# A combined schedule change in a four-layer network kernel: layer 1's turn and MLP begin, and Fourier's row 64, last unit and second copy

## The chip, the cores and the metric

The kernel runs on one core of one Trainium2 chip. The metric is the device time of one execution in microseconds (us); lower is better. Everything is computed in one launch, in float32 unless the reference asks for rounding to a smaller format.

## The reference, cut to what matters

The network has four layers on an image batch of 4 x 96 channels x 64 x 64 (16,384 tokens of 96 channels, 4,096 per image). Layer 0 is a selective state-space block, and layer 2 is a linear attention with a quantised MLP; the change touches neither. Layer 1 and the first half of layer 3 are these:

```python
# layer 1
h = conv_depthwise_7x7(x) + conv_b                 # per channel
h = layer_norm_over_channels(h) * ln_g + ln_b
h = gelu(h @ w1 + b1)                              # 96 -> 384
x = (h @ w2 + b2) * layer_scale + x                # 384 -> 96
# layer 3, first half ("Fourier"); its input is layer-normed, its output added to t
h = relu(bn1(x @ w1.T))                            # 96 -> 192
X = fft(h, axis=tokens, norm="ortho")              # 4096 tokens
xr = relu(X.real * rd - X.imag * idg + rb)
xi = relu(X.imag * rd + X.real * idg + ib)
y = ifft(xr + 1j * xi, axis=tokens, norm="ortho").real
o = bn2(y @ w2.T)                                  # 192 -> 96
```

A second quantised MLP ends layer 3 and the kernel.

## The kernel before, in words

The stages run one after another. Through most of the kernel t, a tile of 96 partitions by 16,384 tokens, stays in SBUF. In layers 1 to 3 the order of instructions on TensorE (PE), VectorE (DVE), ScalarE (ACT) and GpSimd (POOL) is the program's order (a manual schedule). DMAs are issued on SyncE's queue (SP), whose order a planner of the framework sets; a DMA is issued when the queue has come to it and its slot is free. Tiles with a tag share a ring of `bufs` slots.

**Layer 1, the turn.** `tokens` loads 1,024 tokens of layer 0's output (`o`) and of the input (`xr`), scales the one on ACT and adds the other on DVE into t (L737). `turn` brings these tokens from channels on partitions to tokens on partitions: eight blocks of 128 tokens go in as TensorE's weights, and the moving operand is a unit matrix of 96 rows (L744). Four blocks share a PSUM tile, which ACT copies in one half and DVE in the other into xt. There are 16 chunks, and the tokens of a chunk are asked for one chunk ahead.

**Layer 1, the convolution.** It is done with banded matrices, 1 MB for four channels, loaded as `band`, three slots. At the eighth of 24 groups it also prepares constants for the later layers (`consts2`), whose small matmuls use the turn's PSUM ring.

**Layer 1, the MLP.** A block is 512 tokens; there are 32, in eight groups of four. `stats` takes mean and variance on DVE (four rows of 128 tokens per call), `roots` the inverse square root of a group's variances on ACT by Ln and Exp, `back` normalises on DVE and turns the block back on TensorE, `hidden` is the first matrix with Gelu on ACT, `out` the second, added to t on DVE. Ln and Exp, and Gelu, are in different function tables of ACT, and a table load stands between them.

**Fourier.** The transform over 4,096 tokens is split in 32 x 128. A unit is one image and one half of the 192 hidden features, so there are eight units; a unit takes four steps of six groups of features. In step j of the loop, `over_n1(j)` is the first transform (L1139) with the twiddle products on DVE and POOL, `over_n2(j - 1)` the second (L1160 to L1163) with the weights rd and id, `fold(j - 2)` the relu and the folding to frequencies 0 to 63, `over_k2(j - 3)` the first half of the inverse (L1208, L1209), copied by ACT into bt. `over_k1` is the second half (L1230), on blocks of four columns, with a piece of the inverse matrix loaded as gt (256 KB, two slots), a copy of its PSUM tile into ys by ACT (L1232), and `w2` (L1238) adds the product with the second weight to t on DVE. The inverse of a unit starts two units (eight steps) after its forward transform began; a step does two blocks.

Frequency 64 has its own path: `row64` makes that row by two small products and writes it into partition 64 of bt by way of DRAM, as two DMAs, one after the other (d<-r, bt<-d). The inverse of the unit can't start until it has landed.

```python
if (j - 7) % PER == 0 and 0 <= (j - 7) // PER < len(units):
    row64((j - 7) // PER)
```

Beside this, the units of even number prepare the layer norm of the next image (`norm1`, `norm2`), and those of odd number its first matmul with relu (`w1`, into hh, a ring of three slots). For the last image there is nothing more to prepare.

Of the kernel before, what the change touches and what calls it, by code (L numbers as in the profile page):

```python
# [9 lines left out]
F32 = mybir.dt.float32  # L10
# [8 lines left out]
B, C, HW, L = 4, 96, 64, 4096  # L19
# [31 lines left out]
class Net:  # L51
# [661 lines left out]
    def layer1(self, scratch, t):  # L713
# [4 lines left out]
        with ExitStack() as ctx:  # L718
# [4 lines left out]
            with (  # L723
                tc.manual_schedule(engines=engines),
                tc.tile_pool(name="l1a", bufs=1) as wk,
                tc.tile_pool(name="l1ap", bufs=1, space=PSUM) as psum,
            ):
                for at in (slice(0, 2), slice(NR + 2, NR + 4)):
                    nc.gpsimd.memset(xt[:, :, :, at], 0.0)
                def tokens(b, s):  # L730
                    at = slice(b * L + s * T, b * L + (s + 1) * T)
                    o = wk.tile([C, T], F32, name="o", tag="o", bufs=3)
                    nc.sync.dma_start(o, scratch[:, at])
                    xr = wk.tile([C, T], F32, name="xr", tag="xr", bufs=3)
                    nc.sync.dma_start(xr, ins["x"][b, :, s * T : (s + 1) * T])
                    nc.scalar.activation(o, o, AF.Identity, scale=self.osc, bias=self.osh)
                    nc.vector.tensor_add(t[:, at], o, xr)  # L737

                def turn(b, s):
                    for h in range(2):  # L740
                        ps = psum.tile([128, 4, C], F32, name="xt_ps", tag="xt", bufs=4)
                        for d in range(4):
                            a = b * L + s * T + (4 * h + d) * 128
                            nc.tensor.matmul(ps[:, d], t[:, a : a + 128], self.ident[:C, :C], start=True, stop=True)  # L744
                        r = 2 + s * (T // 128) + 4 * h
                        dst = xt[:, :, b, r : r + 4].rearrange("p c r -> p r c")
                        if h:
                            nc.vector.tensor_copy(dst, ps)
                        else:
                            nc.scalar.copy(dst, ps)  # L750

                chunks = [(b, s) for b in range(B) for s in range(NSC)]
                tokens(*chunks[0])
                for k, chunk in enumerate(chunks):
                    if k + 1 < len(chunks):
                        tokens(*chunks[k + 1])
                    turn(*chunk)

                def load(g):
                    w = wk.tile([128, GC, 4, 128], F32, name="band", tag="band", bufs=3)  # L760
                    nc.sync.dma_start(w, ins["band"][g])
                    return w

                def outer(g):

                    x2 = wk.tile([128, 2 * GC, B, NR], F32, name="x2", tag="x2", bufs=3)
                    at = slice(g * 2 * GC, (g + 1) * 2 * GC)
                    nc.gpsimd.tensor_copy(x2[:64], xt[:64, at, :, 4:])
                    nc.gpsimd.tensor_copy(x2[64:], xt[64:, at, :, :NR])
                    return x2  # L770

                def small(rows, cols):
                    ps = psum.tile([128, 4, C], F32, name="w_ps", tag="xt", bufs=4)
                    return ps.rearrange("p a c -> p (a c)")[:rows, :cols]

                x2 = [outer(0)]
                for g in range(C // GC):
                    if g == 8:
                        self.consts2(wk, small)
                    if g % 2 == 0 and g + 2 < C // GC:  # L780
                        x2.append(outer(g // 2 + 1))
                    w = load(g)
                    ps = psum.tile([128, GC, B, NR], F32, name="cv_ps", tag="cv", bufs=4)
                    for d in range(GC):
                        c = g * GC + d
                        for k, j in enumerate((1, 0, 2)):
                            nc.tensor.matmul(
                                ps[:, d], w[:, d, j], xt[:, c, :, 1 + j : 1 + j + NR], start=k == 0, stop=False
                            )
                        nc.tensor.matmul(ps[:, d], w[:, d, 3], x2[g // 2][:, g % 2 * GC + d], start=False, stop=True)  # L790
                    for d in range(GC):
                        c = g * GC + d
                        dst = xt[:, c, :, 2 : 2 + NR]
                        if g % 2:
                            nc.vector.tensor_scalar_add(dst, ps[:, d], cb[:, c : c + 1])
                        else:
                            nc.scalar.activation(dst, ps[:, d], AF.Identity, bias=cb[:, c : c + 1])
# [52 lines left out]
            n = NT // MB // 4  # L850
            with tc.manual_schedule(engines=engines):
                nc.scalar.preload_act_table_set(ACT_EXP_LN)
                for k in range(2):
                    for d in range(4):
                        stats(k, d)
                    roots(k)
                for d in range(4):
                    back(d)
                for k in range(n):
                    for d in range(4):  # L860
                        hidden(4 * k + d)
                        if k + 1 < n:
                            back(4 * k + 4 + d)
                        if k + 2 < n:
                            stats(k + 2, d)
                        if d:
                            out(4 * k + d - 1)
                    if k + 2 < n:
                        nc.scalar.preload_act_table_set(ACT_EXP_LN)
                        roots(k + 2)  # L870
                    out(4 * k + 3)
# [212 lines left out]
    def fourier(self, dram, t, h):  # L1084
# [5 lines left out]
        with ExitStack() as ctx:  # L1090
# [7 lines left out]
            def misc(rows):  # L1098
                return pln.tile([128, MB], F32, name="m_ps", tag="m", bufs=2)[:rows]
# [98 lines left out]
            def over_k2(i):  # L1198

                u, g = its[i]  # L1200
                z = zz.pop(i)
                if g == 0:
                    bt[u] = wk.tile([N1, N2, C], F32, name="bt", tag="bt", bufs=2)
                for e in range(0, G, 3):
                    ps = pln.tile([N1, 3, 128], F32, name="i1_ps", tag="i1", bufs=2)
                    for d in range(3):
                        zd = z[:, e + d].rearrange("p k m -> p (k m)")
                        nc.tensor.matmul(ps[:, d], zd[:, 64:], bc, start=True, stop=False)  # L1208
                        nc.tensor.matmul(ps[:, d], zd[:, :128], bs, start=False, stop=True)  # L1209
                    nc.scalar.copy(  # L1210
                        bt[u].rearrange("p n (g c) -> p g n c", c=4)[:, g + e : g + e + 3],
                        ps.rearrange("p g (n c) -> p g n c", c=4),
                    )

            def row64(u):
# [6 lines left out]
                nc.sync.dma_start(d.rearrange("o (n g c) -> g (o n) c", n=N2, c=4), r)  # L1222
                nc.sync.dma_start(bt[u][64:65].rearrange("p n c -> p (n c)"), d)

            def over_k1(u, n, kept):
                gt = wk.tile([N1, 4, N1], F32, name="gt", tag="gt", bufs=2)
                nc.sync.dma_start(gt, ins["idft"][:, n : n + 4])
                ps = misc(C).rearrange("p (n a) -> p n a", n=4)
                for d in range(4):
                    nc.tensor.matmul(ps[:, d], bt[u][:, n + d], gt[:, d], start=True, stop=True)  # L1230
                kept[u, n] = wk.tile([C, MB], F32, name="ys", tag="ys", bufs=2)
                nc.scalar.copy(kept[u, n], ps.rearrange("p n a -> p (n a)"))  # L1232

            def w2(u, n, kept):

                b, half = units[u]
                ps = misc(C)
                nc.tensor.matmul(ps, self.a_w2[:, half, :], kept.pop((u, n)), start=True, stop=True)  # L1238
                ps = ps.rearrange("p (n a) -> p n a", n=4)
                td = ft[b][:, n : n + 4]  # L1240
# [6 lines left out]
            with tc.manual_schedule(engines=engines):  # L1247
                for n in range(0, N2, 2):
                    w1(0, n)
                kept, sq = {}, {}  # L1250
                for j in range(len(its) + 12):
                    ub, k = divmod(j - 2 * PER, PER)
                    blocks = [(ub, n) for n in (8 * k, 8 * k + 4)] if 0 <= ub < len(units) else []

# [9 lines left out]

                    if j < len(its):
                        over_n1(j)

                    if normed:
                        norm1(b, a, sq)
# [18 lines left out]
                        over_k2(j - 3)  # L1288
                    if normed:
                        norm2(a, sq)  # L1290
                    if (j - 7) % PER == 0 and 0 <= (j - 7) // PER < len(units):
                        row64((j - 7) // PER)
                    turn(len(tokens))
                    if blocks:
                        w2(*blocks[1], kept)
                    if normed and k == PER - 1:
                        norm2(a + MB, sq)


def build(tc, ins, out):  # L1300
# [155 lines left out]
```

## Time and profile before

| | before |
|---|---|
| time, median of 3 runs | 3974.91 us (3973.95 to 3976.82) |
| profiled execution | 3972.29 us, its span 3970.5 us |
| PE, DVE, ACT, POOL busy, whole span | 83%, 79%, 61%, 73% |
| layer 1: turn, convolution, MLP | 2614 to 2670, 2670 to 2791, 2791 to 3014 us |
| Fourier | 3298 to 3838 us |
| last MLP | 3838 to 3970.5 us |

Times inside the execution are counted from the start of the span. "L744" is line 744 of the kernel. A busy TensorE isn't TensorE at its full rate: the profile also gives the clock that was granted to it, as a share of full speed. PEld is the load of weights, which runs beside the matmuls. An idle time of an engine has a releaser, the event that ended it; "issue" is time for which the profile shows no such event.

### The profile page before, as it was taken

How to read it: one execution, taken by the hardware profiler on the slowest of the kernel's cores; microseconds unless marked ns; L12 is line 12 of the kernel's file. 1: busy time of each engine (PE TensorE's matmuls, PEld its weight loads, DVE VectorE, ACT ScalarE, POOL GpSimd, SP SyncE). 2: the span in 40 equal slices, each digit the busy share in tenths (PEclk: the TensorE clock that was granted, in tenths of full speed). 3: DMA queues.
4: the chain of work that ended last, by engine and by line, in shares of the span. 5: the costliest groups of instructions: out<-in, count | busy, mean ns of one | idle time of the engine just before them, and what ended most of it. 6: DMA issues, size and time to landing. Idle time of an engine off the chain costs nothing. (4 is left out here: it accounts for less than half of the span.)

```text
span 3970.5 us, 45322 instructions
## 1 busy us (share of the span) xinstructions
PE 3291.6 (83%) x14174; PEld 1420.1 (36%) x14174; DVE 3155.9 (79%) x2772; ACT 2419.9 (61%) x4644; POOL 2912.9 (73%) x1443
## 2 busy tenths in 40 slices
PE   7888788888888778888878888677899998999878
PEld 3222222222222222222222222167445535666643
DVE  5999999999999999999999999941662384444539
ACT  4676667666666766677666666431345586655548
POOL 2999999999999999999999999911001064534417
PEclk8888888888887888788888888658899999999989
DMA  7567656756675667566666766566000000011111
GB/s 185 135 161 174 144 148 159 175 142 159 160 173 132 164 166 170 132 167 166 159 147 158 170 148 154 120 170 227 11 0 1 1 1 6 22 33 33 43 44 58
DMA packets 183291, 468.12 MB, mean 118 GB/s; under 512 B 53237, under 2 KB 55167, under 8 KB 179969
## 3 DMA queue, kind: packets, MB, share of 16 engines
q1 hardware_dynamic: 183048, 465.21, 47.1%
q8 instruction: 113, 1.85, 0.2%
q14 instruction: 130, 1.06, 0.1%
HBM read 391.53 MB, written 73.50 MB: 117 GB/s over the span
## 5 line engine op out<-in xcount | busy, mean ns | idle before, releaser
L496 POOL TENSOR_TENSOR hs<-hs,crep 128x1024 f32<-128x1024 f32 x768 | 1796.6, 2364 | 27.3 <-DVE hs L490 23.7
L454 PE MATMUL rep<-dbl,sel_b 32*128 32x512 f32 x1152 | 406.1, 781 | 464.1 <-DVE hs L490 433.4
L474 POOL TENSOR_TENSOR up<-udb,brep 128x1024 f32<-128x1024 f32 x256 | 605.1, 2364 | 8.5 <-DMA brep<-cd 8.5
L468 ACT ACTIVATE da<-ddb,nega 128x1024 f32<-128x1024 f32 x512 | 585.0, 1150 | 16.2 <-DVE hs L490 8.2
L468 ACT ACTIVATE dap<-ddb,nega 128x1024 f32<-128x1024 f32 x256 | 286.2, 1118 | 423.7 <-DVE hs L490 421.9
L515 PE MATMUL y<-hs,sel_r 128*32 128x512 f32 x3072 | 483.3, 689 | 6.5 <-POOL hs L496 6.4
L490 DVE TENSOR_TENSOR_SCAN hs<-da,state,rep 128x1024 f32<-128x1024 f32 x192 | 450.8, 2348 | 16.7
L490 DVE TENSOR_TENSOR_SCAN hs<-da,state,u 128x1024 f32<-128x1024 f32 x192 | 450.9, 2348 | 11.2 <-DVE u L486 1.4
L490 DVE TENSOR_TENSOR_SCAN hs<-dap,state,up 128x1024 f32<-128x1024 f32 x192 | 447.0, 2328 | 6.8 <-ACT dap L468 6.8
L454 PEld LDWEIGHTS rep<-dbl,sel_b 32*128 32x128 f32 x1152 | 109.0, 218 | 760.9 <-issue 512.8
L210 PE MATMUL ps<-n,w_x 97*64 97x512 f32 x1536 | 364.8, 617 | 9.4 <-ACT n L323 5.3
L486 DVE TENSOR_TENSOR u<-udb,rep 128x1024 f32<-128x1024 f32 x256 | 314.6, 1229 | 42.5 <-PE rep L454 11.3
L486 DVE TENSOR_TENSOR rep<-udb,rep 128x1024 f32<-128x1024 f32 x256 | 310.6, 1213 | 0.4
L1039 POOL CAST hq<-y 128x1536 fp8e5<-128x1536 f16 x64 | 93.9, 1467 | 253.7 <-issue 144.0
L210 PEld LDWEIGHTS ps<-n,w_x 97*64 97x64 f32 x1536 | 108.9, 140 | 257.5 <-issue 210.9
L515 PEld LDWEIGHTS y<-hs,sel_r 128*32 128x32 f32 x3072 | 66.9, 116 | 363.5 <-issue 195.8
L382 POOL TENSOR_TENSOR du<-delta,xc 128x512 f32<-128x512 f32 x96 | 122.6, 1277 | 67.4 <-ACT delta L366 52.2
L1178 POOL TENSOR_TENSOR av<-av,ec 128x780 f32<-128x780 f32 x32 | 58.8, 1837 | 150.1 <-ACT av L1175 150.1
L224 PE MATMUL ps<-xc,xproj 64*102 64x512 f32 x384 | 160.3, 998 | 3.5 <-ACT xc L344 3.5
L358 ACT COPY dbl<-ps 102x512 f32<-102x512 f32 x64 | 34.4, 589 | 207.1 <-PE ps L224 207.1
L911 POOL MEMSET h<- 1x4096 f32 x1 | 3.5, 3506 | 213.1 <-DVE n L824 213.1
L490 DVE TENSOR_TENSOR_SCAN hs<-da,rep 128x1024 f32<-128x1024 f32 x64 | 146.5, 2289 | 5.4
(256 smaller groups left out, 6492.9 us busy)
## 6 DMA issues: line engine op xcount, KB each, us to landing
ddb<-dd SPq DMA_DIRECT2D x768, 128.0 KB
udb<-ud SPq DMA_DIRECT2D x768, 128.0 KB
crep<-cd SPq DMA_DIRECT2D x512, 128.0 KB
brep<-cd SPq DMA_DIRECT2D x256, 128.0 KB
dd<-delta SPq DMA_DIRECT2D x64, 384.0 KB
ud<-du SPq DMA_DIRECT2D x192, 128.0 KB
band<-in_band SPq DMA_DIRECT2D x24, 1024.0 KB
gt<-in_idft SPq DMA_DIRECT2D x64, 256.0 KB
```

The source lines that it names most:

```text
L210: nc.tensor.matmul(ps[rows], w[:, 64 * p : 64 * p + 64], rhs[:, at.start + shift : at.stop + shift], start=k == 0, stop=k == len(ws) - 1, ...
L224: nc.tensor.matmul(ps, w[rows, p], x[rows, p], start=start and p == 0, stop=p == 2)
L382: nc.gpsimd.tensor_mul(u, m["delta"][:, of], m["xc"][:, of])
L454: nc.tensor.matmul(x[:, at], sel_b[rows, order[t][1]], made[k]["dbl"][rows, at], start=True, stop=True)
L468: nc.scalar.activation(da, made[k]["dd", h, j], AF.Exp, scale=nega[:, col : col + 1])
L474: nc.gpsimd.tensor_mul(u, made[k]["ud", h, j], made[k]["brep", g])
L486: nc.vector.tensor_mul(u, made[k]["ud", h, j], x)
L490: nc.vector.tensor_tensor_scan(hs[:, 1:], made[k].pop(("da", t)), u, 0.0 if s == 0 else st, ALU.mult, ALU.add)
L496: nc.gpsimd.tensor_mul(hs[:, :T], hs[:, 1:], made[k]["crep", order[t][1]])
L515: nc.tensor.matmul(made[k]["y", p][row : row + 32], sel_r, made[k]["hs", t][:, at], start=False, stop=True, skip_group_check=True,)
L1039: nc.gpsimd.tensor_copy(q, y2, saturate=False)
L1178: nc.gpsimd.tensor_add(v[:, 2:4], v[:, 0:2], ec)
```

## The change

Five things are edited:

- the turn's unit matrix is taken with all 128 columns, and its PSUM tiles, like those of the small constants and of `over_k2`, are made four by 128 wide, of which 96 or three parts are read;
- the begin of the MLP: the first group's statistics and roots, one `back`, and then the loop, in which the statistics of the second and third group and the second group's roots are spread over the first four blocks; `back` is now two blocks ahead of `hidden` instead of four;
- `row64` is called one step earlier;
- the last unit's blocks leave the loop; in a loop of their own, `over_k1` of a block comes ahead of `w2` of the block before, and `w2` there uses `over_k2`'s PSUM ring; the inverse matrix is loaded in two halves of 1 MB into slots of hh, and from there on no gt is loaded where a half holds it;
- ys of a step's second block is copied by DVE instead of ACT, but for the last unit.

```diff
 def turn(b, s):
     for h in range(2):
-        ps = psum.tile([128, 4, C], F32, name="xt_ps", tag="xt", bufs=4)
+        ps = psum.tile([128, 4, 128], F32, name="xt_ps", tag="xt", bufs=4)
         for d in range(4):
             a = b * L + s * T + (4 * h + d) * 128
-            nc.tensor.matmul(ps[:, d], t[:, a : a + 128], self.ident[:C, :C], start=True, stop=True)
+            nc.tensor.matmul(ps[:, d], t[:, a : a + 128], self.ident[:C], start=True, stop=True)
...
-                nc.vector.tensor_copy(dst, ps)
+                nc.vector.tensor_copy(dst, ps[:, :, :C])
             else:
-                nc.scalar.copy(dst, ps)
+                nc.scalar.copy(dst, ps[:, :, :C])
...
     nc.scalar.preload_act_table_set(ACT_EXP_LN)
-    for k in range(2):
-        for d in range(4):
-            stats(k, d)
-        roots(k)
     for d in range(4):
-        back(d)
+        stats(0, d)
+    roots(0)
+    back(0)
     for k in range(n):
         for d in range(4):
-            hidden(4 * k + d)
-            if k + 1 < n:
-                back(4 * k + 4 + d)
-            if k + 2 < n:
+            i = 4 * k + d
+            hidden(i)
+            if k == 0 and d == 2:
+                nc.scalar.preload_act_table_set(ACT_EXP_LN)
+                roots(1)
+            for i2 in (1, 2) if i == 0 else (i + 2,):
+                if i2 < 4 * n:
+                    back(i2)
+
+            if k == 0:
+                for d2 in (2 * (d % 2), 2 * (d % 2) + 1):
+                    stats(1 + d // 2, d2)
+            elif k + 2 < n:
                 stats(k + 2, d)
             if d:
-                out(4 * k + d - 1)
+                out(i - 1)
         if k + 2 < n:
             nc.scalar.preload_act_table_set(ACT_EXP_LN)
             roots(k + 2)
...
-    ps = pln.tile([N1, 3, 128], F32, name="i1_ps", tag="i1", bufs=2)
+    ps = pln.tile([N1, 4, 128], F32, name="i1_ps", tag="i1", bufs=2)[:, :3]
...
+late = {}
+
+def fetch(k):
+    g = wk.tile([N1, CG, N2, 4], F32, name="hh", tag="hh", bufs=3)
+    g = g.rearrange("p g n c -> p (g n c)")[:, : N2 // 2 * N1].rearrange("p (n a) -> p n a", n=N2 // 2)
+    nc.sync.dma_start(g, ins["idft"][:, k * N2 // 2 : (k + 1) * N2 // 2])
+    for n in range(0, N2 // 2, 4):
+        late[k * N2 // 2 + n] = g[:, n : n + 4]
+
 def over_k1(u, n, kept):
-    gt = wk.tile([N1, 4, N1], F32, name="gt", tag="gt", bufs=2)
-    nc.sync.dma_start(gt, ins["idft"][:, n : n + 4])
+    if n in late:
+        gt = late[n]
+    else:
+        gt = wk.tile([N1, 4, N1], F32, name="gt", tag="gt", bufs=2)
+        nc.sync.dma_start(gt, ins["idft"][:, n : n + 4])
...
-    nc.scalar.copy(kept[u, n], ps.rearrange("p n a -> p (n a)"))
+    copy = nc.vector.tensor_copy if n % 8 and u < len(units) - 1 else nc.scalar.copy
+    copy(kept[u, n], ps.rearrange("p n a -> p (n a)"))
 
 def w2(u, n, kept):
     b, half = units[u]
-    ps = misc(C)
+    if u < len(units) - 1:
+        ps = misc(C)
+    else:
+        ps = pln.tile([N1, 4, 128], F32, name="i1_ps", tag="i1", bufs=2)[:C].rearrange("p n a -> p (n a)")
...
-for j in range(len(its) + 12):
+for j in range(len(its) + 4):
...
     if j < len(its):
         over_n1(j)
+    if j in (len(its) - 7, len(its) - 3):
+        fetch((j - len(its) + 7) // 4)
...
-    if (j - 7) % PER == 0 and 0 <= (j - 7) // PER < len(units):
-        row64((j - 7) // PER)
+    if (j - 6) % PER == 0 and 0 <= (j - 6) // PER < len(units):
+        row64((j - 6) // PER)
...
+last = [(len(units) - 1, n) for n in range(0, N2, 4)]
+for k, block in enumerate(last):
+    over_k1(*block, kept)
+    if k:
+        w2(*last[k - 1], kept)
+w2(*last[-1], kept)
```

`PER` is 4, the steps of a unit; `its` has the 32 steps of all units.

More of the change, by code (lines that the diff above doesn't have):

```diff
@@ L772, in small @@
                 def small(rows, cols):
-                    ps = psum.tile([128, 4, C], F32, name="w_ps", tag="xt", bufs=4)
+                    ps = psum.tile([128, 4, 128], F32, name="w_ps", tag="xt", bufs=4)
                     return ps.rearrange("p a c -> p (a c)")[:rows, :cols]
```

## The prediction

> **What bounds the kernel now.** I read the page's 40 slices first, then the table by stretches of time, which cuts the one core's span of 3970.5 us into stages: layer 0 to about 2609 us, layer 1 to 3014, layer 2 to 3298, Fourier to 3838, last MLP to the end. The diff touches layer 1 and Fourier only, 405 and 540 us long. In each I looked for time in which TensorE is idle or at half clock. Columns below: stretch, length, busy time of PE, PEld, DVE, ACT, POOL, then granted clock, DMA share, GB/s.
>
> ```profile
> 2614.00:2670.00 56.00, 54.93 (x256) 54.69 (x256) 29.12 (x32) 28.91 (x31) 0.00 (x0) 0.50 0.93 257
> 2630.00:2640.00 10.00, 10.00 (x49) 10.00 (x49) 5.31 (x7) 5.49 (x6) 0.00 (x0) 0.50 1.00 266
> 2770.00:2780.00 10.00, 10.00 (x92) 10.00 (x91) 1.13 (x4) 2.29 (x8) 0.18 (x1) 1.00 0.91 310
> ```
>
> The first two rows are the turn: TensorE without a gap, yet at clock 0.50, and 214.6 ns an instruction (54.93 / 256). The third is the convolution that follows, equally dense, with 128 moving columns where the turn has 96: clock 1.00 and about 110 ns. In the turn's rows DMA is nearly full too.
>
> The MLP's begin, by the timeline of layer 1:
>
> ```profile
> 2790.72 0.32 DVE L810 BATCH_NORM_STATS2 st<-xt 128x6 f32<-128x96 f32 x1
> ...
> 2804.19 1.15 DVE L824 TENSOR_SCALAR n<-xt,mv,rs 128x96 f32<-128x96 f32 x4
> ...
> 2815.79 4.45 PE L838 MATMUL g_ps<-xc,c_w 96*128 96x512 f32 x6
> ```
>
> 25 us pass from the convolution's end to the first hidden matmul, while DVE makes 32 statistics of 0.42 us and four `back`s of 3.1.
>
> Fourier, from TensorE's timeline where the inverse of unit 1 begins:
>
> ```profile
> 3473.48 1.50 PE L1139 MATMUL s_ps<-dft,hh 128*128 128x130 f32 x12
> 3477.94 1.94 PE L1230 MATMUL m_ps<-gt,bt 128*96 128x128 f32 x8 [2.95 <-DMA bt<-d]
> 3495.48 1.50 PE L1139 MATMUL s_ps<-dft,hh 128*128 128x130 f32 x12
> 3510.14 1.50 PE L1139 MATMUL s_ps<-dft,hh 128*128 128x130 f32 x12
> ```
>
> L1139 opens a step of the loop. Steps with the same work take 14.66 us (3495.48 to 3510.14); the one whose inverse waits for row 64's two DMAs takes 22.00: 2.95 us of waiting and then matmuls at half clock. The last unit, in the chain of waits:
>
> ```profile
> 3807.84 4.73 issue
> 3812.57 2.01 PE m_ps L1230 x8
> ...
> 3837.08 1.01 DVE t L1244
> ```
>
> 30.2 us from 3807.84 to the last add's end at 3838.08: the DMAs, a cold start, and eight blocks in single file (2.70 us each once warm).
>
> **The Trainium skill.** "TensorE: Matmul & The Clock Gate", Part 1, What's actually happening: the clock is halved by default and released after about 3.4 us of sustained activity. The convolution and the wait at 3474.99 to 3477.94 agree; the turn, 54.93 us dense and never released, shows that occupancy isn't what is counted. "DMA: Bandwidth & Descriptors", Anatomy of one DMA: about 2.0 us fixed; row 64's 12 KB pieces took 2.93 and 2.39. "ScalarE: Activation LUTs", What ACT_TABLE_LOAD costs: about 1283 ns; the trace has 1.28 us. "PSUM — Partial Sum Buffer", Specifications: a bank is 512 FP32; the tiles of 384 become whole banks, and no wait in this trace is seen to come from their size, so I cost that at nothing, 0 to -1 us.
>
> **Part 1, the turn (moving 96 to 128 columns).** At half clock 128 columns cost what 96 do, within 5 us: the convolution's first cold matmuls run at about 0.21 to 0.25 us. If the clock is released, a chunk's 16 instructions take 1.8 us instead of 3.43 and DMA becomes the limit: the first adds (L737), which waited for loads, start at 2613.30, 2616.35 and 2619.42, so 3.05 us a chunk. The last add then starts at 2613.3 + 15 x 3.05 = 2659, against 2663.4; after it TensorE has 1.8 to 3.4 us and a copy of 0.8, so the turn ends near 2663.5 instead of 2670.4: -7 (0 to -10 with a warm start of the convolution). The bands' loads move with it, as their DMAs follow the last chunk's in SP's queue; the first band's 1 MB at 310 GB/s takes 3.4 us after 2659, just in time. The constants' stall at 2704 to 2729 moves along whole.
>
> **Part 2, the MLP's begin.** `roots(0)` now follows 16 statistics: done at 2800.8 (two table loads of 1.28 and two activations), not 2804.2; the first hidden starts at about 2804.3 instead of 2815.8. But the statistics of groups 1 and 2 now stand between `back`s on DVE's queue: behind them wait copies, then `hidden`, and a table load more, 1.28 us, sits in front of `roots(1)`. Following both queues with these durations, TensorE idles 1.1, 1.9 and 3.4 us, and reaches `hidden(5)` near 2842 instead of 2845.6, with two `back`s (1.7 us) still owed: -2. The gaps may hold the clock down, +2. I take 0, with -4 to +4. Later groups are TensorE-bound (99% busy) with the same work.
>
> **Part 3, row 64 one step earlier.** Its four matmuls, the copy and the two DMAs keep their price and trade steps (0.9 us from one to the other). DMA 5.3 us then lies under a whole step of 11.6 to 14.9. On SP the row's second DMA waits for the first, and the next `gt` load is behind it; the trace has `gt` two blocks ahead, so it is not needed before the DMA has passed. Savings in the first step of each unit's inverse (units 0 to 7), against an undisturbed step: unit 1 (3473.48) 22.0 to 15.4, as ScalarE's chain to the first `ys` is late next, -6.6; unit 3 (3600.70) 21.8 to 15.4, -6.4; unit 5 (3714.88) 15.6 to 11.6, -4.0; unit 6 (3765.9, no L1139 in it) 15.9 to about 10, -6; units 2 and 4, which wait 0.83 and 1.66 us and hide most of it, together -1.2; unit 0 nothing. Sum -24. The last unit's wait is in part 4.
>
> **Part 4, the last unit.** Matmuls of blocks interleave: 0.87 us for L1230 and 0.86 for L1238 when nothing waits (3455.80 to 3456.66; 3503.91 to 3504.78). Eight pairs make 13.9, plus the last add's 1.4: 15.3 instead of 30.2, -15. ScalarE's copy, 0.2 + 0.58, hides under the next block's 0.87; VectorE's add, 1.15, under 1.73. Row 64 lands near 3807, with up to 1 us of wait left. The two 1 MB `fetch`es replace 26 of the 64 `gt` loads of 256 KB; their slots are free at steps 23 and 27 and wanted at 25 and 30. Unseen in the trace: 1 MB here takes 3.4 to 4.1 us at 310 to 257 GB/s plus 2; I take 0, at worst +5.
>
> **Part 5, second copy on VectorE.** 0.69 us (as L831, same size) instead of 0.58 to 0.61 behind twelve `av`s. VectorE then has only the block's add and next step's `p` behind it, and idled 5.3 us there. It spares the waits on `ln_rs` (0.29) and `ys` (0.83, counted in part 3): -2, 0 to -4.
>
> **Sum.** -7 + 0 - 24 - 15 - 2 = -48 on the profiled execution of 3972.29 us (span 3970.5): 3924. That execution lies 2.6 below the median of three, 3974.91; against the median, 3927.
>
> **Rivals.** *The turn stays at half clock* (its 96 rows, not its columns, are the reason, or the threshold lies higher): for it, that occupancy of 98% didn't help; against it, `hidden`, also of 96 rows but 512 columns, warms within 4 us. Time: 3927 + 8 = 3935. *A new wait takes the old one's place*: on SP, a row's second DMA holds back `gt` for the step between, for units 1 to 5, where the old stall cost up to 7 us each with the clock lost: +26, 3953. *Slower*: the same place, if each of those five steps lost more than 48 / 5 = 9.6 us, for instance both blocks stalled and cold, 12 us each: 3987. Against both: eight `gt`s stand between two rows on SP, so two of the coming unit are issued ahead of the row already. *The change doesn't do what it says*: row 64 lands in time anyway for units 2 and 4 (0.83 and 1.66 us of waiting), so for those there's little to gain; counted.
>
> **Chances.** Forecast 0.62, half clock 0.22, new wait 0.12, slower 0.04. Between 0.2% (8 us, about what a measurement of this kernel can tell) on either side lies the worse edge of the new wait, 0.03; faster 0.93, slower 0.04. The range takes the unknown ends of parts 1, 2, 4 and 5 (-12 to +12), the half clock, and most of the new wait: 3906 to 3952.
>
> **What would show it.** In the changed profile: the turn's rows at a clock above 0.7 and its end near 2663; first hidden near 11 us earlier relative to the convolution's end, with gaps after; no `bt<-d` as a releaser of L1230; unit 3's first step near 15 us; L1230 and L1238 alternating at 1.73 us at Fourier's end. It is wrong if L1230 waits for `gt` or `hh` loads, or if the turn stays at 0.50 and Fourier's steps keep their 22 us.

## The result, and the profile after

| | before | after |
|---|---|---|
| time, median | 3974.43 us (3963.18 to 3976.82, 4 runs) | 3930.03 us (3928.55 to 3934.46, 4 runs) |
| ratio to before | | 0.9896, interval 0.9875 to 0.9916 |
| profiled execution, its span | 3972.29, 3970.5 us | 3934.46, 3932.7 us |

The change saves 44.4 us by the medians; the prediction said 48. The profiled execution of after is the slowest of its four, so its trace shows 37.8 us. A second series of runs of the same kernel, further down, gave 3927.67 us. By stages of the two profiled executions:

| stage | before | after | difference |
|---|---|---|---|
| turn, first L744 to first L787 | 55.9 | 52.3 | -3.6 |
| convolution and MLP of layer 1 | 340.8 | 340.5 | -0.3 |
| layer 2, to the first L1139 (after: L1146) | 306.9 | 300.5 | -6.3 |
| Fourier, to the last MLP's first matmul | 520.1 | 492.5 | -27.6 |
| last MLP | 132.4 | 132.6 | +0.2 |

A sum near the forecast hides terms that are not: layer 2, which no line of the diff touches, gave 6.3 us, and Fourier gave 13 us less than was forecast.

From here on Fourier's lines of after have new numbers: L1139 became L1146 (`over_n1`), L1230 is L1250 (`over_k1`), L1232 is L1254 (the copy to ys), L1238 is L1263 (`w2`), L1190 is L1197 (zz, the tile that the fold writes). Layer 1 keeps its numbers. The steps of Fourier's loop are counted from 0. The inverse of unit u begins in step 8 + 4u: step 12 for unit 1, 20 for unit 3, 24 for unit 4. Its row 64 is made in the step before that, and in after one step earlier still (for unit 1 in step 10 instead of 11).

The turn, by stretches of time (columns as in the prediction: stretch, length, busy PE, PEld, DVE, ACT, POOL, granted clock, DMA share, GB/s):

```profile
2614.00:2660.00 46.00, 33.05 (x238) 30.76 (x239) 27.71 (x29) 28.57 (x29) 0.00 (x0) 0.92 1.04 250
2630.00:2640.00 10.00, 6.16 (x48) 5.58 (x48) 6.07 (x7) 5.82 (x6) 0.00 (x0) 1.00 1.04 252
2660.00:2665.00 5.00, 3.48 (x18) 3.29 (x17) 1.93 (x2) 1.62 (x3) 0.00 (x0) 0.70 0.99 408
```

The clock is 0.92 to 1.00 where it was 0.50. PE is now busy for 62% of the middle (6.16 of 10.00) and DMA is full: the bound has moved from TensorE to the loads. In the third row the clock falls again, at the very end.

TensorE's timeline of after, around the turn's end and the MLP's begin (start, length, instruction, idle time before it and its releaser):

```profile
2658.35 2.05 PE L744 MATMUL xt_ps<-ident,t 96*128 96x128 f32 x16 [0.93 <-DVE t L737]
2661.92 3.72 PE L744 MATMUL xt_ps<-ident,t 96*128 96x128 f32 x16 [1.52 <-DVE t L737]
2666.58 1.62 PE L787 MATMUL cv_ps<-xt,band 128*128 128x128 f32 x6 [0.94 <-issue]
...
2799.84 5.49 PE L838 MATMUL g_ps<-xc,c_w 96*128 96x512 f32 x6 [0.78 <-DVE xc L831]
...
2813.12 1.18 PE L829 MATMUL tp_ps<-ident,n 128*96 128x128 f32 x8 [1.93 <-DVE n L824]
...
2822.58 1.99 PE L829 MATMUL tp_ps<-ident,n 128*96 128x128 f32 x8 [3.13 <-DVE n L824]
```

A chunk's 16 matmuls take 2.05 us warm; the last chunk takes 3.72, at half clock. The first hidden matmul (L838) starts 16 us earlier than before, 12 of them relative to the convolution's end, and the gaps of 1.93 and 3.13 us that follow are the price.

Fourier, TensorE's timeline of after: unit 1's first step of the inverse, and the last unit:

```profile
3464.75 1.50 PE L1146 MATMUL s_ps<-dft,hh 128*128 128x130 f32 x12
...
3472.80 1.10 PE L1263 MATMUL m_ps<-ys,a_w2s 96*96 96x512 f32 x2 [3.04 <-ACT ys L1254]
...
3484.87 1.50 PE L1146 MATMUL s_ps<-dft,hh 128*128 128x130 f32 x12
...
3786.34 1.02 PE L1263 MATMUL i_ps<-ys,a_w2s 96*96 96x512 f32 x2
3787.20 1.04 PE L1250 MATMUL m_ps<-hh,bt 128*96 128x128 f32 x8
3788.07 1.03 PE L1263 MATMUL i_ps<-ys,a_w2s 96*96 96x512 f32 x2
```

No instruction of L1250 waits for row 64 any more: in before the line had 13.9 us of waits for `bt<-d` and 7.9 of "issue", in after 0.4 us in all, for something else. But the step from 3464.75 to 3484.87 still takes 20.12 us, and its wait is now 3.04 us for ys. The last unit's blocks alternate every 0.87 us without a wait.

### The profile page after: what moved, and what is told of

It is laid out like the page before. It is cut to its first block, busy times and chain, and to the rows that moved or that the text cites. A ratio compares the mean times of both kernels' runs of the same rounds, so it can differ in the third digit from the quotient of the medians.

```text
span 3932.7 us, 45252 instructions
## 1 busy us (share of the span) xinstructions
PE 3252.8 (83%) x14174; PEld 1392.7 (35%) x14174; DVE 3172.6 (81%) x2800; ACT 2405.3 (61%) x4616; POOL 2911.9 (74%) x1443
## 5 line engine op out<-in xcount | busy, mean ns | idle before, releaser
L224 PE MATMUL ps<-xc,xproj 64*102 64x512 f32 x384 | 150.8, 944 | 3.5 <-ACT xc L344 3.5
```

Source lines behind the costliest of these rows:

```text
L224: nc.tensor.matmul(ps, w[rows, p], x[rows, p], start=start and p == 0, stop=p == 2)
```

## The experiments

Each is compared with the kernel before in runs on the same chip, whose medians lay between 3971.78 and 3973.28 us. Below, "ratio" is to the kernel before. Stage times are of the one profiled execution of each run, so a median and a stage need not agree: they scatter by a few microseconds. One source of it can be seen. In three of the fourteen profiles (the tile, row 64 and the last unit alone) the last MLP, which no edit touches, took 128.1 us; in the others it took 132.2 to 133.7, with the clock at half for 13.7 us or more from just behind its first matmul on. And in six kernels in which nothing in Fourier's loop ahead of its last steps was edited, step 12 took 20.6 to 22.4 us and step 20 20.5 to 21.8.

### The five parts, one at a time

**The turn.** The kernel before with the first part of the diff alone (128 columns, and tiles four by 128 wide):

```diff
...
-    nc.tensor.matmul(ps[:, d], t[:, a : a + 128], self.ident[:C, :C], start=True, stop=True)
+    nc.tensor.matmul(ps[:, d], t[:, a : a + 128], self.ident[:C], start=True, stop=True)
...
```

> The kernel before with the turn's part alone (128 moving columns, PSUM tiles four by 128). Theory (the clock is released by the wider moving operand, DMA is the next limit): turn's clock above 0.9, its end about 4 us earlier as in the changed kernel, last chunk and the convolution's first matmuls still at half clock; whole time -3 to -8 us. Rival (the 6.3 us that layer 2 lost from its begin in the changed kernel came with the turn or the tiles): layer 2 shorter by 6 us here as well, whole time -10 us. Rival (chance of the clock's window): layer 2 as long as in one of the two kernels, with no relation to the edit.

3962.57 us, ratio 0.9974 (0.9967 to 0.9981). The turn took 51.7 us instead of 55.9, at clock 0.91 to 1.00; layer 2 took 306.9, as before. The medians differ by 9.2 us, a little more than expected, the stage by 4.2; this profiled execution (3969.84) lay above its median, and where the other 5 us of the medians lie it doesn't show.

**The tile alone.** Tiles four by 128 wide, still 96 columns:

```diff
-    ps = psum.tile([128, 4, C], F32, name="xt_ps", tag="xt", bufs=4)
+    ps = psum.tile([128, 4, 128], F32, name="xt_ps", tag="xt", bufs=4)
...
-    nc.tensor.matmul(ps[:, d], t[:, a : a + 128], self.ident[:C, :C], start=True, stop=True)
+    nc.tensor.matmul(ps[:, d, :C], t[:, a : a + 128], self.ident[:C, :C], start=True, stop=True)
...
```

> The kernel before with the turn's PSUM tiles four by 128 wide but the unit matrix still of 96 columns, to part the tile's size from the columns. Theory (only the columns streamed per weight load release the clock): turn at 0.50 throughout and 56 us long, time as before. Rival (the bank's alignment lets it go): turn at 0.9 and more, 4 us shorter.

3971.1 us, ratio 0.9997 (0.9988 to 1.0006). The table by stretches for this kernel:

```profile
2614.00:2668.00 54.00, 53.62 (x252) 53.38 (x251) 28.48 (x31) 27.59 (x31) 0.00 (x0) 0.50 0.92 259
```

TensorE is as dense as before and never leaves half clock. So the number of moving columns released the clock in the turn, not the tile's size. The release isn't firm: in three of the seven profiles with 128 columns the clock fell once more for 6.8 us in the middle of the turn.

**The MLP's begin.** The kernel before with the second part of the diff alone.

> The kernel before with the MLP's begin alone. Theory (the statistics only move between the backs, and TensorE's gaps eat what the earlier start brings): layer 1's end within 1 us of the kernel before, whole time within 3 us but for layer 2's begin. Rival (the earlier start is worth its 12 us, and another part of the changed kernel spoilt it): layer 1 shorter by 8 us or more.

3965.41 us, ratio 0.9985 (0.9978 to 0.9991). From the turn's start to layer 2's first matmul it took 396.2 us against 396.6 in before: nothing. Layer 2 took 300.5 us instead of 306.9, which is all that the edit can be seen to gain.

**Row 64.** One step earlier, nothing else:

```diff
-    if (j - 7) % PER == 0 and 0 <= (j - 7) // PER < len(units):
-        row64((j - 7) // PER)
+    if (j - 6) % PER == 0 and 0 <= (j - 6) // PER < len(units):
+        row64((j - 6) // PER)
```

> The kernel before with row 64 one step earlier alone, the copy still on ScalarE. Theory (the wait goes everywhere, but in the first steps of units 1 and 3 VectorE's fold, held up by GpSimd, is late next): no bt<-d before the inverse's matmuls, those two steps 18 to 20 us instead of 22.0 and 21.8, units 5 and 6 shorter by 4 and 5.5, the last unit by 5 to 7; Fourier -18 to -22 us. Rival (the early DMA or the queue's order costs elsewhere): steps with row 64 in them longer by more than the 0.9 us that it takes; Fourier -10 or less.

3954.59 us, ratio 0.9956 (0.9941 to 0.9971). Fourier took 500.3 us, 19.8 less. Units 5 and 6 gained what was expected; unit 1's first step (step 12) went only from 22.00 to 20.08, unit 3's (step 20) from 21.82 to about 18.5.

**The last unit.** The loop of its own and the two `fetch`es, with row 64 and the copy as before.

> The kernel before with the last unit's part alone (loop of its own, two fetches, PSUM ring of over_k2), row 64 and the copy as before. Theory (overlap of blocks, 0.97 us each, the row's DMA wait of 5 us staying in front): Fourier's tail 30.3 to about 22 us, nothing else; -7 to -9 us. Rival (the fetches collide with gt or wait for hh): steps 25 to 30 longer than 11.6 us, and less gained.

3961.2 us, ratio 0.9975 (0.9964 to 0.9986). From the last `over_n1` to Fourier's end it took 77.3 us instead of 84.5, as expected; Fourier as a whole gained only 4.8. The profiled execution lies 11.1 us below that of before, but 4.3 of these are the last MLP's shorter time, and 2.4 lie ahead of the turn. A new cost showed: step 24 took 14.23 us instead of 12.00, with a wait of 2.19 us for `bt<-d`; the first 1 MB fetch had been issued 11.7 us ahead of row 64's first DMA. In the changed kernel, whose row comes a step earlier, step 24 takes 11.58.

**The copy.** The second block's ys by VectorE, nothing else:

```diff
-    nc.scalar.copy(kept[u, n], ps.rearrange("p n a -> p (n a)"))
+    copy = nc.vector.tensor_copy if n % 8 and u < len(units) - 1 else nc.scalar.copy
+    copy(kept[u, n], ps.rearrange("p n a -> p (n a)"))
```

> The kernel before with the second copy on VectorE alone. Theory (that copy was never late): Fourier within 2 us of before, the 0.29 us waits for ln_rs perhaps gone. Rival (it also shortens the first step of units 1 and 3, where w1's PSUM slot waited for it): those two steps 1 us shorter each.

3967.8 us, ratio 0.999 (0.9983 to 0.9996); Fourier 517.1, -2.9. Steps 12 and 20 went to 19.56 and 19.79 although row 64 was as late as ever. TensorE's timeline of this kernel in step 12:

```profile
3476.79 1.99 PE L1230 MATMUL m_ps<-gt,bt 128*96 128x128 f32 x8 [3.32 <-DMA bt<-d]
```

The wait for row 64 is even longer than before's 2.95 us. So the copy and the row seem to shorten partly the same step, and their savings can't be added there. The amount is unsure: 19.56 and 19.79 lie 1.1 and 0.7 us under the lowest of the six kernels named above.

By the medians the five parts alone save 9.2, 6.4, 17.2, 10.6 and 4.5 us, 47.8 together, which by their intervals is unsure by about 9; the whole change saved 44.4. By the stages that the parts change they save 4.2, 6.4, 19.8, 4.8 and 2.9 us, 38.1 together, against 37.8 between the profiled executions of before and after. So no loss between the parts can be seen; the question was why row 64 brought so much less than 24.

### Why the first steps of units 1 and 3 stay long

In this stretch GpSimd and ACT still finish the layer norm of the next image (ln_rs is its scale, h the tokens that GpSimd multiplies by it), while the transform goes on: f is made by two GpSimd additions, av goes through the relu on ACT, zz is the fold on DVE. The trace of after, all engines in step 12:

```profile
3466.24 0.68 ACT L1121 ACTIVATE ln_rs<-m_ps,eps 96x512 f32<-96x512 f32 x1 [1.82 <-POOL h L1123]
...
3467.50 0.84 ACT L1192 ACTIVATE av<-av 128x780 f32<-128x780 f32 x1
...
3467.67 1.27 POOL L1123 TENSOR_TENSOR h<-h,ln_rs 96x512 f32<-96x512 f32 x1 [1.46 <-ACT ln_rs L1122]
...
3468.45 2.72 DVE L1197 SCALAR_TENSOR_TENSOR zz<-av 128x384 f32<-128x384 f32 x1 [0.25 <-ACT av L1192]
...
3468.90 1.85 POOL L1158 TENSOR_TENSOR f<-p,p 128x390 f32<-128x390 f32 x2
...
3471.17 0.55 DVE L1197 SCALAR_TENSOR_TENSOR zz<-av 128x384 f32<-128x384 f32 x1
...
3471.75 0.52 ACT L1203 ACTIVATE zz<-zz 128x384 f32<-128x384 f32 x1 [3.41 <-DVE zz L1197]
3472.18 0.56 ACT L1254 COPY ys<-m_ps 96x512 f32<-96x512 f32 x1
```

Read it upwards from the copy to ys, for which TensorE waits (3472.80). ACT stood 3.41 us for the first zz. That zz took 2.72 us; the next one, of the same shape, 0.55. The long one began while GpSimd multiplied h and ended 0.4 us after GpSimd's f (3468.90 + 1.85 = 3470.75) was done. The relu on av, and GpSimd's h, were so late because ACT's second Ln had stood 1.82 us: ln_rs has one slot, and GpSimd still read the first. The Trainium skill, "SBUF — State Buffer", SBUF: two separate sides, says that VectorE and GpSimd share a pair of ports as an exclusive lock, which a VectorE operation with two SBUF inputs contends for. zz has two (two parts of av). The trace agrees: each of the twelve zz of after that took over 1 us ended 0.41 or 0.42 us after the end of a GpSimd operation. It wasn't always the last of a run: in steps 2 to 4 zz began within h too, took 1.57 to 1.75 us and ended after the first of the two f. Why it came in there and not in steps 12 and 20 isn't known.

In before the same zz was short:

```profile
3474.14 0.68 ACT L1114 ACTIVATE ln_rs<-m_ps,eps 96x512 f32<-96x512 f32 x1 [1.69 <-POOL h L1116]
...
3475.56 1.27 POOL L1116 TENSOR_TENSOR h<-h,ln_rs 96x512 f32<-96x512 f32 x1 [1.46 <-ACT ln_rs L1115]
...
3476.84 0.55 DVE L1190 SCALAR_TENSOR_TENSOR zz<-av 128x384 f32<-128x384 f32 x1
```

The Ln stood nearly as long (1.69 us), but zz began just when h was over. What changed is TensorE's place. Step 12 began at 3473.48 in before and at 3464.75 in after, so h began 2.08 us into it in before and 2.92 in after. Counted from the begin of step 11 it is the same, 18.91 and 18.89 us: step 11 has lost row 64 and takes 15.97 us instead of 16.83, TensorE is 0.86 us earlier in step 12, and GpSimd isn't. That moved zz from the end of h into h. In the kernel with only row 64 moved step 11 takes 15.97 us too, and zz takes 2.72 in steps 12 and 20.

Two theories were put to the test: the place of zz against GpSimd's h and f, or ACT's queue with the one slot of ln_rs. Two experiments on the changed kernel.

**The fold ahead of `over_n1`** in the first steps concerned, so that zz is issued ahead of f:

```diff
+    first = not k and b < B and u % 2 and 2 <= j < len(its) + 2
+    if first:
+        fold(j - 2)
     if j < len(its):
         over_n1(j)
...
-    if 2 <= j < len(its) + 2:
+    if 2 <= j < len(its) + 2 and not first:
         fold(j - 2)
```

> The changed kernel, but in the first step of units 1, 3 and 5 of the loop that also make w1 the fold stands ahead of the twiddle products in the program. Theory (VectorE's fold is held for GpSimd's additions f, since they start before it): fold takes 0.55 us instead of 2.7 there, w2 waits under 1 us instead of 3.0, TensorE keeps its clock, the two steps 15 to 17 us instead of 20.1 and 17.8; -4 to -7 us. Rival (the wait comes from ScalarE's queue, Ln and Exp ahead of the relu): fold waits all the same for the relu, p and f come later, time unchanged or 2 us longer.

3920.15 us, ratio 0.9866 (0.985 to 0.9882). Steps 12 and 20 took 16.34 and 16.35 us; Fourier 482.7, 9.8 less than in after. zz still began within h, but with no f behind h it took 0.90 us (not the 0.55 expected), and TensorE's wait for ys was 1.25 us (not under 1). The time is 7.5 to 9.9 us under the two series of the changed kernel, more than the -4 to -7 expected. About half of Fourier's 9.8 us lies in these two steps: step 4, which the edit reaches too, and steps 7 and 8 give 3.8 us of the rest.

**ln_rs in two slots** (r64 gives up its second slot for the space):

```diff
-    rs = wk.tile([C, MB], F32, name="ln_rs", tag="rs")
+    rs = wk.tile([C, MB], F32, name="ln_rs", tag="rs", bufs=2)
...
-    r = wk.tile([CG, N2, 4], F32, name="r64", tag="r64", bufs=2)
+    r = wk.tile([CG, N2, 4], F32, name="r64", tag="r64")
```

> The changed kernel with two slots instead of one for norm2's ln_rs, so that ScalarE's last Ln doesn't wait for GpSimd's multiplication (r64 is cut to one slot to make room). Theory (GpSimd's lock is what counts): relu comes 1.4 us earlier in the first steps of units 1 and 3, but VectorE is at its products then, so little changes: 0 to -2 us. Rival (ScalarE's queue is the cause): those steps lose 1.5 us and their cold matmuls, -4 us or more.

3920.07 us, ratio 0.9869 (0.9854 to 0.9883). Steps 12 and 20 took 15.90 us each; Fourier 482.4. My expectation, 0 to -2, missed; the size is that of its rival (ScalarE's queue), -4 or more. Step 4, with the same arrangement, gave 2.4 us more. The same step in this kernel's timeline, all engines:

```profile
3458.11 0.69 ACT L1121 ACTIVATE ln_rs<-m_ps,eps 96x512 f32<-96x512 f32 x1 [0.58 <-PE m_ps L1119]
3459.53 1.27 POOL L1123 TENSOR_TENSOR h<-h,ln_rs 96x512 f32<-96x512 f32 x1 [0.18 <-ACT ln_rs L1122]
3461.21 0.55 DVE L1197 SCALAR_TENSOR_TENSOR zz<-av 128x384 f32<-128x384 f32 x1
3461.43 2.44 POOL L1158 TENSOR_TENSOR f<-p,p 128x390 f32<-128x390 f32 x2 [0.63 <-DVE p L1150]
3464.07 1.10 PE L1263 MATMUL m_ps<-ys,a_w2s 96*96 96x512 f32 x2 [1.23 <-ACT ys L1254]
```

The Ln waits 0.58 us instead of 1.82, h is over by 3460.80, and zz begins 0.22 us ahead of f and takes 0.55; this time f is the longer one (2.44 for the two, not 1.85). So the two theories are one chain: the slot brings h forward, from 2.92 us into the step to 1.69, and zz is clear of h again. Both remedies do one thing: zz no longer stands behind h and f both. (r64's second slot went in the same edit; no run parts the two.)

**Both remedies**, and the changed kernel beside them:

> The changed kernel with both remedies: ln_rs in two slots, and the fold ahead of over_n1 in the first steps of the inverse of units 1, 3 and 5's predecessors. If ScalarE's late queue and GpSimd's hold of VectorE are one chain (theory), each remedy alone has already broken it: steps 12 and 20 stay at 15.9 to 16.4 us, and the time lies within 4 us of either remedy alone, some 10 us below the changed kernel of this same call. If they were two separate losses (rival), the gains would add up: 15 to 20 us below the changed kernel, with steps 12 and 20 near 14 us.

> The changed kernel once more, beside the version with both remedies and against the kernel before: 0.989 to 0.990 of it, with steps 12 and 20 at 20.1 and 17.8 us.

Both together 3920.16 us, ratio 0.9872 (0.9857 to 0.9887); the changed kernel 3927.67, ratio 0.9889 (0.9874 to 0.9903). Steps 12 and 20 took 15.07 us with both; in the changed kernel 18.35 and 18.58, so the two steps vary between executions (20.12 and 17.75 in the first), and again a zz of 2.72 us stands in each. The zz alone doesn't make the spread: in the first execution step 12 had 6.8 us of half clock and step 20 none, in this one each had 3.4; with either remedy there was none. The gains don't add up in the time. In the steps they do in part: 15.07 is 0.8 under the 15.9 expected at the least, but steps 7 and 8, 12.02 and 13.98 us with the fold first, stand at 13.31 and 15.34 again. Why they do isn't known.

### Where layer 2's 6.3 us come from

Six kernels without the new begin of the MLP (before, the turn alone, the tile alone, row 64 alone, the last unit alone, the copy alone) show a mean clock of 0.57 to 0.59 from 3010 to 3030 us, around the border to layer 2, and 306.8 to 306.9 us for the layer. The six kernels with it keep 1.00 there. The new begin has two sides: the statistics in the loop, and `back` two blocks ahead instead of four, which also moves the last `back`. So, the kernel before with the second side alone:

```diff
-    for d in range(4):
+    for d in range(2):
         back(d)
...
-    if k + 1 < n:
-        back(4 * k + 4 + d)
+    if 4 * k + d + 2 < 4 * n:
+        back(4 * k + d + 2)
```

> The kernel before, with its own begin of the MLP (both groups' statistics and roots first), but back two blocks ahead of hidden instead of four. It asks where layer 2's 6.3 us come from. If the end of layer 1's MLP is the cause (theory: with two ahead, turns of 96 columns stand until two blocks before the border, with four ahead only 512-column matmuls in the last four), layer 2 takes 300.5 us instead of 306.8, its first 16 us at clock 1.00, and the time is 0.9983 to 0.9986 of before. If the begin is the cause by way of something else (rival), layer 2 stays at 306.8 us with clock 0.50 after the border, and the time is within 2 us of before.

3959.05 us, ratio 0.9968 (0.9955 to 0.998). The table by stretches around the border, first before, then this kernel:

```profile
3012.00:3016.00 4.00, 3.26 (x5) 0.69 (x4) 0.17 (x1) 1.91 (x3) 4.00 (x2) 0.72 0.00 0
3016.00:3020.00 4.00, 3.32 (x5) 0.96 (x4) 0.52 (x1) 1.70 (x3) 1.41 (x1) 0.50 0.00 0
3020.00:3030.00 10.00, 9.32 (x19) 4.27 (x19) 1.66 (x3) 4.50 (x8) 0.00 (x0) 0.50 0.00 0
```

```profile
3012.00:3016.00 4.00, 2.94 (x7) 1.02 (x8) 0.79 (x2) 1.79 (x3) 1.24 (x1) 1.00 0.00 0
3016.00:3020.00 4.00, 3.81 (x18) 2.08 (x17) 0.69 (x1) 3.06 (x6) 0.00 (x0) 1.00 0.00 0
3020.00:3030.00 10.00, 10.00 (x64) 6.80 (x63) 2.06 (x3) 6.93 (x13) 0.00 (x0) 1.00 0.01 2
```

Layer 2 takes 299.6 us with the clock kept, 7.2 less than in before. That this edit keeps it is shown. The theory given for it, the kind of matmuls ahead of the border, is not: in both kernels the clock is 1.00 up to the border, and the first waits behind it are the same, 0.84 us for t and 0.74 for sq.

The traces point to where in time these waits fall. In layers 1 and 2 of all fourteen profiles each stretch at half clock is a whole multiple of 3.41 us (3.41 to 68.3 us, 75 stretches), so the clock changes on a grid of that step. The first table below begins with the stretch of the grid that holds both waits in before. The second is the stretch of the grid, in the kernel with two `back`s, in which TensorE is busy least (its grid is carried on from the clock's last change, at 2812.6):

```profile
3010.37:3013.78 3.41, 1.83 (x5) 0.65 (x5) 0.75 (x1) 0.59 (x1) 3.33 (x1) 1.00 0.00 0
3013.78:3030.85 17.07, 15.70 (x30) 6.36 (x29) 2.75 (x4) 8.10 (x13) 3.62 (x2) 0.50 0.00 0
```

```profile
3010.61:3014.02 3.41, 2.21 (x5) 0.57 (x4) 0.69 (x1) 2.16 (x5) 2.63 (x1) 1.00 0.00 0
```

In before TensorE is busy for 54% of that stretch (1.83 of 3.41), and the clock falls as it ends; in the other kernel it is 65% (2.21), and the clock stays. In all six kernels that lose the clock the stretch ahead of the fall has 54 to 58%; in the eight that keep it no stretch in the first 16 us behind the border is under 62%. The border's place on the grid follows from the edit: from the last rise of the clock in the MLP to the border it takes 191.8 to 192.2 us in the six, 181.2 to 181.4 with the new begin and 194.4 with the old one and two `back`s. On this reading an edit that moves the end of the MLP by a fraction of 3.41 us decides on these 6 to 7 us. It is argued from the profiles and not shown: no run moves the border alone. Nor is 60% a rule: at the border to the last MLP the clock fell after a stretch of 60% in one kernel and stayed through stretches of 57% in two others.

This run brought a second thing that was not expected. TensorE's timeline at the MLP's begin:

```profile
2805.64 1.99 PE L829 MATMUL tp_ps<-ident,n 128*96 128x128 f32 x8 [15.30 <-DVE n L824]
2808.68 2.02 PE L829 MATMUL tp_ps<-ident,n 128*96 128x128 f32 x8 [1.05 <-DVE n L824]
2810.49 3.81 PE L838 MATMUL g_ps<-xc,c_w 96*128 96x512 f32 x6
...
2839.68 2.74 PE L838 MATMUL g_ps<-xc,c_w 96*128 96x512 f32 x6
```

The first hidden matmul comes 10.7 us later than in after, but no gap follows, and the sixth (2839.68) is where after has it (2839.74), though this kernel's convolution ended 5.3 us later. From the convolution's last matmul to layer 2 it takes 217.0 us against 222.1 in before and 222.2 in after: the old order of statistics with two `back`s beats the new begin by 5.

### The best version

The changed kernel with ln_rs in two slots and this begin of the MLP in place of the changed one:

> The changed kernel with ln_rs in two slots and, in place of the changed begin of the MLP, the begin of before with back two blocks ahead. If the parts add up: layer 1 from the turn's start to layer 2's first matmul some 4 us shorter than in the changed kernel (388 us against 392.8), layer 2 at 299.6 to 300.5 us, Fourier at 482 us as with two slots alone, 3914 to 3917 us in all, some 12 us below the changed kernel. If the two slots' gain hung on the changed begin (no mechanism seen), it stays near 3920 us.

3917.31 us, ratio 0.9864 (0.9848 to 0.9881). Layer 1 from the turn's start to layer 2 took 385.6 us (389.4 in the second series of the changed kernel), layer 2 299.7, Fourier 483.9. It has the lowest median of all that ran, 10 us under that series' 3927.67 and just above the 3914 to 3917 expected. But the ratios to before were taken on different chips, and the intervals overlap, a little with the changed kernel's (0.9874 to 0.9903) and almost wholly with those of one remedy.

## Why the prediction was right or wrong, step by step

- **Part 1, the turn: right in kind, about half in size in the profiled execution.** The clock was released and DMA became the bound, as said; -3.6 us instead of -7. The term that failed is the period of a chunk: adds start at 2613.05 and 2660.65, 47.60 / 15 = 3.17 us, not the 3.05 that I took from three starts; that is 1.8 us. The rest is at the end: 5.9 us from the last add to the convolution, not 4.5. The bands' loads, issued at 2653.19, share the DMA with the last chunk's (the last add came 3.58 us after the one before, which came after 2.98), and TensorE had cooled by then, the "3.4 us" end of what I allowed. Across executions of the changed kernel and its variants the stage took 49.0 to 52.3 us, -3.6 to -6.8. The rival that the turn stays at half clock fell, and the reading that occupancy isn't what is counted held: with 98% occupancy and 96 columns it stays at 0.50, with 62% and 128 columns it runs at 1.00.
- **Part 2, the MLP's begin: right in layer 1, blind for layer 2.** In layer 1 it was worth nothing, with the forecast gaps of 1.1, 1.9 and 3.4 us measured as 1.14, 1.93 and 3.13 (`hidden(5)` came 1.6 us earlier against the convolution's end, not 3.6). The failing step is the sentence that the diff touches layer 1 and Fourier only: the new begin changed the clock of the next layer, 6.3 us, most likely by where in time the MLP ends.
- **Part 3, row 64: right for units 5 and 6, wrong for 1 and 3.** No wait on `bt<-d` is left. Unit 5's step went from 15.58 to 11.57 (-4.0, as forecast), unit 6's -5.5 (forecast -6). Unit 1's saved 1.9 (forecast 6.6), unit 3's 4.1 (6.4). The failing step is "trade steps (0.9 us from one to the other)", which was taken as a price that cancels. The 15.4 is ScalarE's chain as it lay in before, where zz took 0.55 us. But the 0.9 us out of step 11 bring TensorE that much earlier to step 12 and leave GpSimd's h where it was; so zz fell into h and lasted 2.72 us, and matmuls at half clock followed in three of the four such steps of the two executions. Clear of h, with the two slots, these steps take 15.90, close to the 15.4. A small term was missed too: unit 0's row now stands in step 6, which has less other work; steps 6 and 7 together grew from 24.83 to 26.49 us, +1.7. The rival of a wait for `gt` on SP fell: no L1250 waits for it.
- **Part 4, the last unit: right.** From 30.2 to 16.2 us, -14.1 (forecast -15), in pairs of 1.73 us. The `fetch`es, costed at 0, cost nothing that shows in the changed kernel (the 2 us in their price are what the Trainium skill, "DMA: Bandwidth & Descriptors", Anatomy of one DMA, gives for DMAs issued by GpSimd; these are issued on SyncE, where row 64's took 2.93 and 2.39); with the row a step later (the last unit alone) step 24 grew by 2.2 us, within the "at worst +5".
- **Part 5, the copy: about right alone, nothing seen to be added in the sum.** Alone it gave 2.9 us in Fourier's profile, inside the 0 to -4 (4.5 by the medians), in the very steps that row 64 lengthens. In the change no step is left over in which it shows.
- **The sum.** Fourier was forecast at -41 and gave -27.6. Missing are 4.7 and 2.3 us on units 1 and 3, 1.7 on unit 0, 2 on the copy, about 1 each on the last unit and on units 2 and 4, 0.5 on unit 6. Layer 2's 6.3 us, which nothing in the prediction saw, made up for half of it. So that the total came to 3930 against 3927 is in part luck: two errors of opposite sign.

## What to carry to other kernels

When a wait is removed, price the chain that is late next with the operations as they run beside their new neighbours. Even 0.9 us of work taken out of one step shifts one engine against another in the next: here it moved a fold of 0.55 us into GpSimd's run of instructions, where it took five times as long, and one slot more in a small buffer, or an earlier place in the order, undid it. Price an early start by where the sixth block is, not the first: work moved from ahead of the loop into it came back as gaps, while shortening the lookahead gained. And look at the granted clock behind the borders of a stage, too, when only the order inside it is changed: a gain that hangs on where in time a border falls, as layer 2's 6 us seem to, can be lost by the next edit ahead of it.

## What the runs showed of the hardware that was not expected

- The same VectorE operation (scalar_tensor_tensor, 128 x 384, float32) took 0.54 to 0.56 us in 52 of its 64 places in after. In the other twelve it ended 0.41 or 0.42 us after the end of a GpSimd operation and took 1.17 to 1.75 us, and 2.72 and 2.73 where two more followed that it came in behind.
- TensorE at 98% occupancy with 96 moving columns per load of weights stayed at clock 0.50 for 54 us; with 128 columns and less occupancy it ran at 0.92 to 1.00.
- The clock changed on a grid of 3.41 us in layers 1 and 2. Behind the same two waits of 0.84 and 0.74 us at a border the clock fell, for 6 to 7 us of loss, where TensorE was busy for 54 to 58% of the stretch of the grid that held them, and stayed where no stretch was under 62%. Elsewhere in the same traces shares near 60% went both ways, so the rule behind it is open.
